# A graph layer's hot rows in three runs of matrix products, and the y products of a block's two parts in alternation

## The chip, the cores and the metric

The kernel runs on one core of a Trainium2 chip. The metric is the device time of one execution in microseconds (us). Before the change three runs took 3902.74, 3901.97 and 3891.67 us; the median is 3901.97.

The core's engines are TensorE (in the profile PE, with its weight loads PEld), VectorE (DVE), ScalarE (ACT), GpSimd (POOL) and SyncE (SP). Each takes its own instructions in order and waits on semaphores for the others. [...]

## The reference

A graph of 12,500 nodes with 128 features each and 412,500 edges, sorted by destination (every edge in both directions and one loop per node).

```python
theta = x[dst] - x[src]
w = sigmoid(relu(theta @ W1 + b1) @ W2 + b2)
agg = segment_sum(w * theta, dst)
indeg = segment_sum(ones, dst)
x = layernorm(x + agg + indeg * (x @ W4 + b4))
```

W1 and W4 are 128x128, W2 is 128x1. All is fp32.

## The kernel before, in words

**Tables.** A first stage computes `x @ W1` for all nodes into the DRAM table `z`, which holds `[x @ W1 | x]` per node, and `x @ W4 + b4` into `u_d`.

**Parts and blocks.** The edges are cut into parts of some 1,400 in the order of their destinations; the first 26 parts (`PLAIN`) have 1,024 edges and a simpler path (`early_part`, L1274). Two parts make a block (`SUB = 2`); h = 0 is its even part, h = 1 its odd one. 138 blocks come after the plain ones. The destinations of a part lie in a window of 48 nodes, those of a block in 96.

**Three kinds of work for a part.**

- *Gathered rows.* For most edges POOL gathers the source's row of `z`, 128 edges at a time: eight indirect DMAs for a part into one of seven `zbuf` buffers (`gather`, L362; DMA at L373). The destination's side `y = x[dst] @ W1 + b1` needs no gather: a one-hot matrix `oh` (48 nodes and one row for b1, in a half of 64 partitions) times the window's rows. That is `spread_y`, L845, with its matmul at L861: four products of 64 rows for a part, into one PSUM buffer `y`. There are two such buffers. VectorE then takes `y - z` (L895), the relu with W2 (L900) and the sum (L906); this is `logits`, L880.
- *Hot rows.* Edges whose source lies among the first 6,144 nodes can, up to 16 per part and table of 256 nodes, be served without a gather: the tables lie in SBUF (`tabs`), ScalarE builds a one-hot `of` from a list of their numbers (`hot_tiles`, L977; L983 and L985), and TensorE multiplies tables by one-hots (`hot_products`, L987; L997) into `pd`, which ScalarE copies to `xT_all` (`hot_out`, L1003; L1011). One such step serves four tables for eight parts; six steps fall on eight parts, so that every even part has one, and every second odd part.
- *Hot rows of a block* (`hot_rows`, L1027). From `xT_all`, where the hot edges' source rows stand transposed, TensorE makes for six tiles of 128 edges (three for each part) both `x` and the logit's operand `y - x @ W1`. `wni` is `[-W1 | identity]`, 128x256: one product with it (L1037) writes `[-x @ W1 | x]` side by side, and a second one (L1041) adds the destination's `y` from `oh`. The first part's y product uses its 64 rows; the second's uses all 128 rows, with a copy of the window's rows (`y2b`) whose first half is zero. Four of the six tiles lie in the PSUM tile `px` of two banks, two in `pz` (`hot_px`, L1021). VectorE reads the first half of each tile (`hot_logits`, L1044; L1050), ScalarE weighs the second (`hot_weights`, L1056; L1061).

**Sums.** `add_block` (L1103; matmul at L1083) adds a block's weighted rows to its 96 nodes by further one-hots, 30 instructions of TensorE, and carries what belongs to the next block. An fp32 product is two matmul instructions in the profile, each with a weight load; a transpose is one.

**The order** is written out by hand in `part(s)`, L1345, since TensorE, VectorE and ScalarE run their instructions in the order of the code there. For TensorE:

- even part of block b: y products of the first part of block b+1 (`spread_ahead`, L1336), `add_block(b - 1)`, hot products;
- odd part of block b: y products of the second part of block b+1, hot products if it has any, `hot_rows(b + 1)`.

ScalarE rebuilds `of` for the next hot products at the end of a part (`fetch_step`, L1257), after it has weighed that part's rows (L947), and only once the last hot products have read `of`.

**The gathers' pace.** `spread_ahead` also issues the gathers of part s + 3. The first of the eight waits for `newest[0]`, TensorE's latest product of a kind that records itself there when the gather is issued: `hot_rows`, `hot_products` and the sums do, `spread_y` doesn't. So in an even part the gathers wait for the block's last hot-row product, and in an odd part for the last product of the even part.

Of the kernel before, what the change touches and what calls it, by code (L numbers as in the profile page):

```python
# [9 lines left out]
F32 = mybir.dt.float32  # L10
# [69 lines left out]
def gnn_resnorm(  # L80
# [606 lines left out]
    with tc.manual_schedule(engines={SP}), tc.tile_pool(name="work", bufs=2) as wp, tc.tile_pool(  # L687
# [157 lines left out]
        def spread_y(s):  # L845

            d = parts[s]
            d["y"] = []
            for k0 in range(0, K if s < PLAIN else J, J):
                y = y_tile() if s < PLAIN - 1 else ps_y.tile([P, G, D], F32, name="y")  # L850
                d["y"].append(y)
                if s < NH:
                    px = wide().rearrange("p (k e) -> p k e", e=P)
                    for j in range(J):
                        nc.tensor.transpose(px[:, j, :], rows_of(s)[:, k0 + j, :], ident)
                    xT = next_xT()
                    nc.scalar.activation(xT, px[:, :J, :], AF.Copy)
                if NH <= s < PLAIN:
                    nc.tensor.matmul(y, away_i, rows_of(s)[:, k0:k0 + J, :D], start=True, stop=False)
                for j in range(J if s < PLAIN else pairs(s)):  # L860
                    last = nc.tensor.matmul(y[:, j, :], d["oh"][:, (k0 + j) * P:(k0 + j + 1) * P],  # L861
                                     y_of(s), start=not NH <= s < PLAIN,
                                     stop=s >= PLAIN or s >= NH and j == J - 1)
                    if s < NH:
                        last = nc.tensor.matmul(y[:, j, :], xT[:, j, :], wneg, start=False, stop=True)
            return last

# [153 lines left out]
        def hot_px(b, q):  # L1021

            n = 2 * P * G // (2 * D)
            t = (blocks[b]["px"] if q < n else pz).rearrange("p (q i d) -> p q i d", i=2, d=D)
            return t[:, q % n]

        def hot_rows(b):  # L1027

            s = b * SUB
            blocks[b]["px"] = wide()  # L1030
            j = (s - PLAIN) % HX
            xT = xT_all[:, j:j + SUB, :]
            for h in range(SUB):
                for q in range(HQ):
                    to = hot_px(b, h * HQ + q)
                    at = slice(q * P, (q + 1) * P)
                    nc.tensor.matmul(to, xT[:, h, at], wni, start=True, stop=False)  # L1037
# [3 lines left out]
                    newest[0] = nc.tensor.matmul(to[:, 0, :], oh[:, BP + q * P:BP + (q + 1) * P], y,  # L1041
                                                 start=False, stop=True)

        def hot_logits(b):  # L1044
# [3 lines left out]
            for q in range(SUB * HQ):  # L1048
                h = wp.tile([P, D], F32, name="hh", bufs=1)
                nc.vector.scalar_tensor_tensor(  # L1050
                    h, hot_px(b, q)[:, 0, :], 0.0, w2_r, op0=OP.max, op1=OP.mult,
# [4 lines left out]
        def hot_weights(b):  # L1056
# [3 lines left out]
            for q in range(SUB * HQ):  # L1060
                nc.scalar.activation(wx[:, q, :D], hot_px(b, q)[:, 1, :], AF.Copy, scale=wx[:, q, D:D + 1])  # L1061
# [212 lines left out]
        def early_part(s):  # L1274
# [24 lines left out]
            for t in range(s + 1, s + 2 if s + 1 < PLAIN else s + 3):  # L1299
                spread_y(t)  # L1300
# [35 lines left out]
        def spread_ahead(s):  # L1336

            if s + 2 < NS:
                spread_y(s + 2)
                if PLAIN + AHEAD <= s + 3 < NS:  # L1340
                    if s >= PLAIN + 4:
                        paced[s + 3] = newest[0]
                    gather(s + 3)

        def part(s):  # L1345
# [28 lines left out]
            if h == 1 and b + 1 < NK:  # L1374
                hot_rows(b + 1)
# [236 lines left out]
```

## Time and profile before

| | |
|---|---|
| median of three runs | 3901.97 us |
| profiled execution, its own time | 3876.16 us |
| its span, first to last instruction | 3874.4 us |
| mean granted TensorE clock | 0.80 |
| HBM read, written | 406.12 MB, 27.33 MB |
| DMA engines, mean over the span | 113 GB/s |

The profiled execution is one run of its own; the three timed runs stand beside it.

How to read the lines that follow. A line of a timeline has the start and the length in us, the engine, the line of the kernel, the operation with output and inputs, the shape and the count of instructions merged, and in brackets the idle time of the engine before it with what ended it. "issue" is time in which the engine waited for nothing that the profile shows, "remote" a release whose source the profile cannot name. A line of the waits has who waited for whom, and then the us in total, the number of times and the longest. Matmuls are pipelined, so the next one starts before the length of the last is over: differences of starts tell what one costs. A shape such as 64\*128 is 64 rows of weights by 128 columns, followed by the moving operand. PE is listed with its matmuls alone; weight loads run beside them.

### The profile page before, as it was taken

The page shows a single profiled execution, that of the slowest core. Times are in us where ns is not written, and L with a number is a line of the kernel's source. Part 1 is how long each engine was busy: PE and PEld are TensorE (multiplying, and loading weights), DVE is VectorE, ACT ScalarE, POOL GpSimd, SP SyncE. Part 2 cuts the span into 40 slices and gives each one's busy share as a digit, 9 for nine tenths or more (in the row PEclk, how much of TensorE's full clock was granted, in tenths as well). Part 3 has the DMA queues.
Part 4 walks back from the last instruction along what each step waited for, and adds up shares of the span by engine and source line. Part 5 has one row for each costly group of instructions (what it writes and reads, how often), then busy time and mean ns, then how long its engine had stood idle before and what let it go on. Part 6 is the DMA issues. An engine that isn't in the chain of part 4 may idle for free.

```text
span 3874.4 us, 54748 instructions
## 1 busy us (share of the span) xinstructions
PE 3062.4 (79%) x14964; PEld 2380.6 (61%) x14964; DVE 2567.2 (66%) x5694; ACT 2126.0 (55%) x5542; POOL 2322.7 (60%) x2421
## 2 busy tenths in 40 slices
PE   6786578787888878888888877788887887888887
PEld 5564466666666666666666666666666666666665
DVE  6445257776776776777657776776577777765555
ACT  5454455555555555555555554556555555565553
POOL 5444436666666666666666666666666666666663
PEclk9686778877778877878887778888888878788877
DMA  7332224443444434444444433444444444444432
GB/s 270 106 105 76 80 71 111 112 113 107 115 114 122 115 108 110 111 116 113 115 123 112 111 109 107 117 115 116 117 115 112 110 110 116 114 115 115 116 110 65
DMA packets 259984, 437.28 MB, mean 113 GB/s; under 512 B 69817, under 2 KB 177800, under 8 KB 258132
## 3 DMA queue, kind: packets, MB, share of 16 engines
q0 software_dynamic: 114752, 312.11, 29.0%
q1 hardware_dynamic: 142946, 115.19, 10.8%
q10 hardware_dynamic: 1970, 6.40, 0.5%
q8 instruction: 121, 1.98, 0.2%
q14 instruction: 195, 1.60, 0.1%
HBM read 406.12 MB, written 27.33 MB: 112 GB/s over the span
## 4 chain that ended last, share of the span: by engine, by line
PE 48%; ACT 16%; issue 14%; another core or an unknown queue 13%; DVE 7%; POOL 1%; DMA 1%; SPq 0%; DVEq 0%; POOLq 0%; ACTq 0%
PE pa L1083 10%; PE pd L997 10%; PE px L1037 9%; PE px L1041 5%; PE y L861 5%; ACT of L983 3%; PE pz L1037 3%; ACT of L985 2%; ACT wxh L1061 2%; ACT wx L947 2%; PE pz L1041 2%; ACT xT L1011 1%; DVE hh L1050 1%; DVE zbuf L895 1%
## 5 line engine op out<-in xcount | busy, mean ns | idle before, releaser
L373 POOL DMA_INDIRECT zbuf<-z,src_i x2204 | 2117.7, 961 | 1319.8 <-issue 516.8
L997 PE MATMUL pd<-of,tabs 128*128 128x128 f32 (+1 forms) x3392 | 587.0, 333 | 341.9 <-ACT xT L1011 175.9
L997 PEld LDWEIGHTS pd<-of,tabs 128*128 128x128 f32 x3392 | 534.9, 243 | 380.1 <-ACT xT L1011 194.6
L940 DVE TENSOR_TENSOR wx<-zbuf,fix 128x512 f32<-128x512 f32 x276 | 189.3, 686 | 686.8 <-ACT fix L912 665.4
L983 ACT ACTIVATE of<-hot_src,nodes 128x512 f32<-128x512 f16 (+2 forms) x424 | 281.7, 701 | 654.5 <-remote 327.4
L861 PE MATMUL y<-y,oh 64*128 64x128 f32 x2484 | 467.1, 321 | 212.3 <-issue 180.7
L1083 PE MATMUL pa<-wx,ow 128*96 128x260 f32 (+1 forms) x2620 | 597.8, 380 | 37.3 <-issue 34.8
L861 PEld LDWEIGHTS y<-y,oh 64*128 64x128 f32 x2484 | 368.9, 214 | 319.0 <-issue 252.9
L1037 PE MATMUL px<-wni,xT 128*128 128x256 f32 x1104 | 537.8, 580 | 10.0 <-issue 5.0
L1083 PEld LDWEIGHTS pa<-wx,ow 128*96 128x96 f32 x2620 | 412.9, 170 | 171.4 <-issue 42.4
L1011 ACT ACTIVATE xT<-pd 128x512 f32<-128x512 f32 (+7 forms) x347 | 131.5, 415 | 457.8 <-remote 268.5
L1041 PEld LDWEIGHTS px<-y,oh 64*128 64x128 f32 (+1 forms) x1104 | 237.4, 252 | 229.9 <-issue 213.6
L947 ACT ACTIVATE wx<-zbuf,wx 128x128 f32<-128x128 f32 x1100 | 349.5, 388 | 0.0
L895 DVE TENSOR_TENSOR zbuf<-y,zbuf 128x1024 f32<-128x1024 f32 (+1 forms) x276 | 336.4, 1219 | 13.5 <-PE y L861 7.8
L900 DVE SCALAR_TENSOR_TENSOR zbuf<-zbuf,fix 128x1024 f32<-128x1024 f32 (+1 forms) x277 | 336.5, 1215 | 10.7 <-DVE zbuf L895 0.8
L906 DVE TENSOR_REDUCE lg<-zbuf 128x8 f32<-128x1024 f32 (+1 forms) x277 | 334.6, 1208 | 4.8 <-issue 0.2
L1041 PE MATMUL px<-y,oh 64*128 64x128 f32 (+1 forms) x1104 | 335.5, 395 | 1.7 <-issue 1.1
L1037 PEld LDWEIGHTS px<-wni,xT 128*128 128x128 f32 x1104 | 231.8, 261 | 99.3 <-issue 60.2
L373 POOL DMA_INDIRECT zbuf<-z,src x144 | 137.1, 952 | 152.8 <-ACT wx L930 111.8
L1050 DVE SCALAR_TENSOR_TENSOR hh<-px,w_r 128x128 f32<-128x128 f32 x552 | 160.1, 290 | 100.7 <-PE px L1041 60.8
L985 ACT ACTIVATE of<-of 128x1024 f32<-128x1024 f32 (+2 forms) x212 | 219.7, 1036 | 6.5
L1083 PE MATMUL pa<-wxh,owh 128*96 128x130 f32 x1656 | 208.9, 274 | 17.4 <-issue 17.4
(266 smaller groups left out, 4181.0 us busy)
## 6 DMA issues: line engine op xcount, KB each, us to landing
zbuf<-z,src_i POOLq DMA_INDIRECT x2204
to_all<-off_d SPq DMA_DIRECT2D x276, 112.0 KB
hot_src<-hot_s SPq DMA_DIRECT2D x182, 128.0 KB
z<-zbuf SPq DMA_DIRECT2D x12, 1024.0 KB
xw<-in_x_dram SPq DMA_DIRECT2D x151, 48.0 KB
u<-u_d SPq DMA_DIRECT2D x151, 48.0 KB
out_dram<-o SPq DMA_DIRECT2D x151, 48.0 KB
y<-z SPq DMA_DIRECT2D x294, 24.0 KB
```

The costliest lines, as they stand in the source:

```text
L373: ins = nc.gpsimd.indirect_dma_start(out=rows_of(s)[:, k, :], out_offset=None, in_=z if s >= NH else x, in_offset=IndirectOffsetOnAxis(ap= ...
L861: last = nc.tensor.matmul(y[:, j, :], d["oh"][:, (k0 + j) * P:(k0 + j + 1) * P], y_of(s), start=not NH <= s < PLAIN, stop=s >= PLAIN or s ...
L895: nc.vector.tensor_sub(half, yy.to_broadcast([P, 2, n, D]), half)
L900: nc.vector.scalar_tensor_tensor(h[:, at, :], h[:, at, :], 0.0, w2.to_broadcast([P, n, D]), op0=OP.max, op1=OP.mult)
L906: nc.vector.tensor_reduce(lg[:, at, 0], h[:, at, :], AX.X, OP.add)
L947: nc.scalar.activation(wx[:, k, :D], rows_of(s)[:, k, D:], AF.Copy, scale=wx[:, k, D:D + 1])
L983: nc.scalar.activation(of[:, t, :], hot_src[:, i % NU, :w], AF.Abs, bias=nodes[:, t:t + 1])
L985: nc.scalar.activation(of, of, AF.Relu, scale=-1.0, bias=1.0)
L997: newest[0] = nc.tensor.matmul(to[:, q], tabs[:, g * RG + q, t, :], of[:, t, q], start=t == 0, stop=t == HT - 1)
L1037: nc.tensor.matmul(to, xT[:, h, at], wni, start=True, stop=False)
L1041: newest[0] = nc.tensor.matmul(to[:, 0, :], oh[:, BP + q * P:BP + (q + 1) * P], y, start=False, stop=True)
L1083: newest[0] = nc.tensor.matmul(to if len(w.shape) == 3 else to[:, 0, :], one, w, start=first and i == 0, stop=last and i == len(terms) - 1)
```

## The change

Two things are rearranged on TensorE; VectorE's, ScalarE's and POOL's instructions stay the same in number and size.

- `hot_rows` no longer goes tile by tile. It runs all six x tiles as transposes of `xT_all`, then the six W1 products (128x128), then the six y products. All y products use 64 rows now, and the two parts take turns, tile by tile. The PSUM layout changes with it: the first part's logit operands lie in one bank of `px`, the second's in the other; four x tiles lie in `pz`, and one in what is left of each bank of `px`.
- `spread_y` serves the plain parts alone. `spread_pair(b + 1)` makes the y products of both parts of a block, taking turns, into both `y` buffers; it stands in the odd part of block b, between the hot products and `hot_rows`. The gathers stay where they were.

```diff
@@ spread_y, now for the plain parts alone
-            for k0 in range(0, K if s < PLAIN else J, J):
+            for k0 in range(0, K, J):
...
+        def spread_pair(b):
+
+            ys = []
+            for h in range(SUB):
+                y = ps_y.tile([P, G, D], F32, name="y")
+                parts[b * SUB + h]["y"] = [y]
+                ys.append(y)
+            for j in range(J):
+                for h, y in enumerate(ys):
+                    s = b * SUB + h
+                    if j < pairs(s):
+                        nc.tensor.matmul(y[:, j, :], parts[s]["oh"][:, j * P:(j + 1) * P], y_of(s),
+                                         start=True, stop=True)
...
-        def hot_px(b, q):
-
-            n = 2 * P * G // (2 * D)
-            t = (blocks[b]["px"] if q < n else pz).rearrange("p (q i d) -> p q i d", i=2, d=D)
-            return t[:, q % n]
+        def hot_y(b, h, q):
+            return blocks[b]["px"][:, h * P * G + q * P:h * P * G + (q + 1) * P]
+
+        def hot_x(b, i):
+
+            if i < G:
+                return pz[:, i * P:(i + 1) * P]
+            return hot_y(b, i - G, HQ)
...
@@ hot_rows
-            for h in range(SUB):
-                for q in range(HQ):
-                    to = hot_px(b, h * HQ + q)
-                    at = slice(q * P, (q + 1) * P)
-                    nc.tensor.matmul(to, xT[:, h, at], wni, start=True, stop=False)
-                    oh, y = parts[s + h]["oh"], y_of(s + h)
-                    if h:
-                        oh, y = blocks[b]["oh"], blocks[b]["y2b"]
-                    newest[0] = nc.tensor.matmul(to[:, 0, :], oh[:, BP + q * P:BP + (q + 1) * P], y,
-                                                 start=False, stop=True)
+            tiles = [(h, q) for h in range(SUB) for q in range(HQ)]
+            for i, (h, q) in enumerate(tiles):
+                nc.tensor.matmul(hot_x(b, i), xT[:, h, q * P:(q + 1) * P], ident,
+                                 start=i % G == 0 or i > G, stop=False, is_transpose=True, skip_group_check=True)
+            for h, q in tiles:
+                nc.tensor.matmul(hot_y(b, h, q), xT[:, h, q * P:(q + 1) * P], wneg,
+                                 start=False, stop=False, skip_group_check=True)
+            for q in range(HQ):
+                for h in range(SUB):
+                    newest[0] = nc.tensor.matmul(
+                        hot_y(b, h, q), parts[s + h]["oh"][:, BP + q * P:BP + (q + 1) * P],
+                        y_of(s + h), start=False, stop=True, skip_group_check=True)
...
@@ hot_logits, hot_weights: read hot_y(b, *divmod(q, HQ)) and hot_x(b, q)
...
@@ early_part, at the last plain part: spread_pair(PLAIN // SUB) for two spread_y
...
         def spread_ahead(s):
 
-            if s + 2 < NS:
-                spread_y(s + 2)
-                if PLAIN + AHEAD <= s + 3 < NS:
-                    if s >= PLAIN + 4:
-                        paced[s + 3] = newest[0]
-                    gather(s + 3)
+            if PLAIN + AHEAD <= s + 3 < NS:
+                if s >= PLAIN + 4:
+                    paced[s + 3] = newest[0]
+                gather(s + 3)
...
@@ part
             if h == 1 and b + 1 < NK:
+                spread_pair(b + 1)
                 hot_rows(b + 1)
```

More of the change, by code (lines that the diff above doesn't have):

```diff
@@ L1298, in early_part @@
             logits(s)
-            for t in range(s + 1, s + 2 if s + 1 < PLAIN else s + 3):
-                spread_y(t)
+            if s + 1 < PLAIN:
+                spread_y(s + 1)
+            else:
+                spread_pair(PLAIN // SUB)
             gate_sums(s)
```

11 lines of the change are left out of this document (5 added, 6 removed).

## The prediction

> **What bounds the kernel now.** The first view is the head of the page: the span, and the busy time of the engines.
>
> ```profile
> span 3874.4 us, 54748 instructions
> PE 3062.4 (79%) x14964; PEld 2380.6 (61%) x14964; DVE 2567.2 (66%) x5694; ACT 2126.0 (55%) x5542; POOL 2322.7 (60%) x2421
> ```
>
> No engine is full, so the order of waits decides. A block past the plain ones has two parts, and each part issues eight gathers on POOL. The first gather of an even part (h = 0) waits for the last hot-row product of the block; the first gather of an odd part (h = 1) waits for the last product of the even part, in most parts a hot product (L997). The waits of POOL, and POOL's timeline over one block (start, length, count, idle time before and its releaser):
>
> ```profile
> POOL zbuf L373 <- issue: 556.5, 1802, 1.9
> POOL zbuf L373 <- PE pz L1041: 262.7, 97, 45.7
> POOL zbuf L373 <- remote: 196.1, 90, 2.7
> POOL zbuf L373 <- PE pd L997: 177.6, 43, 6.8
> ```
>
> ```profile
> 1912.09 0.94 POOL L373 DMA_INDIRECT zbuf<-z,src_i  x1 [2.04 <-PE pz L1041]
> 1913.34 0.95 POOL L373 DMA_INDIRECT zbuf<-z,src_i  x1 [0.30 <-issue]
> ...
> 1920.84 0.95 POOL L373 DMA_INDIRECT zbuf<-z,src_i  x1 [0.30 <-issue]
> 1923.88 0.94 POOL L373 DMA_INDIRECT zbuf<-z,src_i  x1 [2.10 <-remote]
> ...
> 1932.69 0.95 POOL L373 DMA_INDIRECT zbuf<-z,src_i  x1 [0.30 <-ACT oh L837]
> 1936.03 0.94 POOL L373 DMA_INDIRECT zbuf<-z,src_i  x1 [2.40 <-PE pz L1041]
> ```
>
> The gathers start 1.25 us apart (1912.09, 1913.34), eight of them end 9.7 us after the first (1920.84 + 0.95), and POOL then waits 2.0 to 2.4 us. This block takes 1936.03 - 1912.09 = 23.94 us, of which 20 are gathers. So what the change can give is bounded by those gaps, 4 us in 24, however much it takes from TensorE.
>
> TensorE's timeline over the same block, and ScalarE's:
>
> ```profile
> 1911.37 1.16 PE L861 MATMUL y<-y,oh 64*128 64x128 f32 x8
> 1912.46 3.75 PE L1083 MATMUL pa<-wx,ow 128*96 128x260 f32 x16
> ...
> 1917.60 1.95 PE L997 MATMUL pd<-of,tabs 128*128 128x128 f32 x16
> 1919.39 0.60 PE L676 MATMUL px<-wni,ew 128*128 128x128 f32 x4
> ...
> 1922.01 0.58 PE L861 MATMUL y<-y,oh 64*128 64x128 f32 x3 [0.82 <-issue]
> 1926.62 3.78 PE L997 MATMUL pd<-of,tabs 128*128 128x128 f32 x16 [4.03 <-ACT xT L1011]
> 1930.20 0.89 PE L1037 MATMUL px<-wni,xT 128*128 128x256 f32 x2
> ...
> 1931.44 0.70 PE L1037 MATMUL px<-wni,xT 128*128 128x256 f32 x2
> ...
> 1932.48 0.70 PE L1037 MATMUL px<-wni,xT 128*128 128x256 f32 x2
> ...
> 1934.28 0.60 PE L1037 MATMUL pz<-wni,xT 128*128 128x256 f32 x2
> ...
> 1934.94 0.60 PE L1037 MATMUL pz<-wni,xT 128*128 128x256 f32 x2
> ...
> 1935.68 0.49 PE L861 MATMUL y<-y,oh 64*128 64x128 f32 x2
> ```
>
> ```profile
> 1923.61 1.33 ACT L983 ACTIVATE of<-hot_src,nodes 128x512 f32<-128x512 f16 x2 [7.58 <-remote]
> ```
>
> The even part's hot products are issued by 1919.39, but ScalarE, which rebuilds `of` for the next ones, starts only at 1923.61, and POOL at 1923.88: about 1.8 us after the eighth gather ended (1921.79), whatever TensorE did. Then ScalarE, 16 hot products (to 1930.20) and the hot rows (5.48 us, to 1935.68) stand in a row, and the next gather follows at 1936.03. In this odd part the hot rows end last.
>
> **What the change removes and adds.** A tile of the first part of a block, with 64 rows, takes 1932.48 - 1931.44 = 1.04 us; one of the second, with 128 rows, 1934.94 - 1934.28 = 0.66. The products are as many, so 0.38 is what going to 64 rows and back costs. [...]
>
> At the full clock an instruction of 128 columns takes 0.112 us (16 in 1919.39 - 1917.60 = 1.79), a 64-row one no less (8 in 1912.46 - 1911.37 = 1.09, mode changes in it), and a transpose, which is one instruction where a product is two, about the same (the four of L676 fill 0.60). After the change the hot rows are 6 transposes, 12 instructions of W1 and 12 of y, with one change in and out: 30 x 0.112 + 0.38 = 3.7 us, or 3.1 if the halves overlap, against 3 x 1.04 + 3 x 0.66 = 5.1. The y products of both parts are 16 x 0.112 + 0.38 = 2.2 us, or 1.3 overlapped, against two runs of 8 x 0.112 + 0.38 = 1.28. TensorE saves 1.8 to 3.3 us a block, 240 to 455 us in 138 blocks. I take the middle of the overlap: hot rows 3.4, y pair 1.75.
>
> Where that lies on the path differs with the odd part. **With hot products in it** (half of the 138): the second part's y products used to stand where TensorE waited for ScalarE anyway (to 1922.59); they now come after the hot products, ahead of the hot rows, with the first part's beside them. The stretch from 1930.20 to the end becomes 1.75 + 3.4 = 5.15 for 5.48, with ends of 4.4 and 5.9. How much of an earlier end reaches POOL, another block shows:
>
> ```profile
> 1339.32 0.94 POOL L373 DMA_INDIRECT zbuf<-z,src_i  x1 [5.66 <-PE pd L997]
> ...
> 1348.08 0.95 POOL L373 DMA_INDIRECT zbuf<-z,src_i  x1 [0.30 <-ACT of L983]
> 1351.19 0.94 POOL L373 DMA_INDIRECT zbuf<-z,src_i  x1 [2.17 <-PE y L861]
> ```
>
> ```profile
> 1348.38 0.39 PE L1041 MATMUL pz<-y,oh 128*128 128x128 f32 x2
> ```
>
> The hot rows ended at 1348.77, before the eighth gather did, and the next gather still came at 1351.19, 11.87 us after the first; above it was 12.15. So the gain is capped at 0.28; I take 0.25: 69 x 0.25 = 17 us.
>
> **Without hot products** the odd part has TensorE at half its clock:
>
> ```profile
> 2091.29 1.22 PE L1037 MATMUL px<-wni,xT 128*128 128x256 f32 x2
> ...
> 2101.04 1.34 PE L861 MATMUL y<-y,oh 64*128 64x128 f32 x8
> ...
> 2107.71 0.27 PE L997 MATMUL pd<-of,tabs 128*128 128x128 f32 x1
> ...
> 2114.01 2.95 PE L997 MATMUL pd<-of,tabs 128*128 128x128 f32 x13 [1.73 <-issue]
> ```
>
> ```profile
> 2091.25 0.94 POOL L373 DMA_INDIRECT zbuf<-z,src_i  x1 [2.04 <-remote]
> ...
> 2101.85 0.95 POOL L373 DMA_INDIRECT zbuf<-z,src_i  x1 [0.30 <-issue]
> ...
> 2117.23 0.94 POOL L373 DMA_INDIRECT zbuf<-z,src_i  x1 [5.42 <-PE pd L997]
> ```
>
> The hot rows take 9.75 us there (2091.29 to 2101.04); at doubled prices the new ones take 6.0 to 7.3, the pair 2.4 to 4.2. They end earlier. But this very case shows the trap: they ended before the eighth gather, POOL went on without a gap, and the hot products of the next part stalled until the second eight were through; the two parts took 25.98 us instead of 23.94. POOL's waits for L997 count such cases: 43 waits at the usual 2.1 would be 90 us, there are 177.6, and the excess of 87 at 5.42 - 2.1 each makes 26 of 69. Mean now: (26 x 25.98 + 43 x 23.94) / 69 = 24.7. After the change all 69 may run so, but the eight y products ahead of the stalled hot products are gone, so eight fewer of these are left behind the stall, at 2.95 / 13 = 0.23 each: 25.98 - 1.8 = 24.2. Gain 0.5 x 69 = 35 us; the cost of that cover, if the 1.8 does not come, is the rival below.
>
> VectorE's L895 needs those y products and used to run 5 us before the hot rows were done; it now waits for the pair.
>
> ```profile
> 1930.28 1.23 DVE L895 TENSOR_TENSOR zbuf<-y,zbuf 128x1024 f32<-128x1024 f32 x1
> ...
> 1939.40 1.22 DVE L895 TENSOR_TENSOR zbuf<-y,zbuf 128x1024 f32<-128x1024 f32 x1
> ```
>
> ```profile
> DVE wx L940 <- ACT fix L912: 665.4, 138, 12.2
> ```
>
> Behind it in VectorE's queue stand the rest of the logits, the hot logits, and through them ScalarE's weights. At worst it starts at 1935.4, 5.1 us later. VectorE's later idle time for the gate is 665.4 / 138 = 4.8 us a block, so this is just covered; I cost it at nothing, and at 0.3 us a block if it is not. The pair itself waits for the odd part's L895, which frees the second y buffer: that ran at 1939.40, 3.4 us after the even part's first gather, and the hot rows began 18.1 us after it (1930.20 - 1912.09), so up to 14 us are left. Behind the pair on TensorE stand the hot rows, and for them wait the next gathers. What the DMA queues issue does not change; the gathers stay paced by the same products.
>
> **Sum.** 17 + 35 = 52 us, from the profiled 3876.2 to 3824. The median of the runs, 3902.0, is 25.8 above the profiled execution, so 3850.
>
> **The rivals.** (1) *All is hidden* behind the 11.9 us between first gathers: 3902, within 12 us of it. For it speaks the block of 1339; against it the 26 long cases. (2) *The gathers run through*, slower: the hot rows end before the eighth gather in all 69 odd parts without hot products, and the next hot products stall as at 2107.71 to 2116.96 with nothing saved. Price 69 x (25.98 - 24.7) = 88 us: 3990. It decides from hot rows that end under 9.7 us after the first gather. (3) *The halves do not overlap* and the change does not do what its second part says: 5.9 for 5.48 in the odd parts with hot products, 69 x 0.42 = 29 us later, and nothing won elsewhere: 3931. (4) *TensorE is the bound after all*, since it holds 48% of the chain on the page:
>
> ```profile
> PE 48%; ACT 16%; issue 14%; another core or an unknown queue 13%; DVE 7%; POOL 1%; DMA 1%; SPq 0%; DVEq 0%; POOLq 0%; ACTq 0%
> ```
>
> Then 240 us or more come back: 3660. Against it stand 20 us of gathers in 23.94. (5) *The clock stays at half* through a run that opens with six transposes: hot rows of at least 6.0 us for 5.48 in the odd parts with hot products, 36 us or more: 3940. Against it, 3.6 us of hot products and the pair come right before the transposes. [...]
>
> **Chances.** My forecast 0.39; (1) 0.13; (2) 0.18; (3) 0.15; (4) 0.10; (5) 0.05. A measurement of this kernel can tell about 0.3% from no change, 12 us. Faster: 0.39 + 0.10 = 0.49; same 0.13; slower 0.38. The likeliest case alone spans 3800 to 3885. The range must take in (2), (3) and (5) as well: 3780 to 3990, and leaves out (4) and the edges.
>
> **What would show it.** Hot rows of 3.1 to 3.7 us where the clock is full; a y pair under 1.9 (overlap) or of 2.2 (none); first gathers 11.9 us apart after odd parts with hot products; POOL's waits for L997 of about 3.6 us, not 5.4. The prediction is wrong if POOL's gaps grow, if VectorE's wait for the y pair reaches the gate, or if blocks come under 22 us.

## The result, and the profile after

Over 20 runs each, the kernel after the change takes 3885.8 us (3870.49 to 3893.3) and the kernel before 3903.39 us (3891.67 to 3916.84): a ratio of 0.9951, with a 95% interval of 0.994 to 0.9963. A second set of runs gave 3886.73 us against 3901.84, 0.9967 (0.9952 to 0.9983). So the change takes some 15 to 18 us away where 52 were forecast. The direction was right, and the size about a third.

The head of the page after the change, and its chain of waits by engine:

```profile
span 3875.8 us, 56094 instructions
PE 2445.5 (63%) x15792; PEld 2080.0 (54%) x15792; DVE 2570.0 (66%) x5694; ACT 2136.0 (55%) x5542; POOL 2324.0 (60%) x2421
DVE 29%; another core or an unknown queue 23%; ACT 16%; issue 15%; PE 13%; POOL 2%; DMA 2%; DVEq 0%; SPq 0%; POOLq 0%; ACTq 0%
```

TensorE's busy time fell by 3062.4 - 2445.5 = 617 us, more than any step of the prediction gave it, and its share of the chain from 48% to 13%. The span did not move: 3874.4 and 3875.8 us. The chain now names "an unknown queue" for 23%. The waits after the change:

```profile
POOL zbuf L373 <- remote: 399.5, 180, 3.2
POOL zbuf L373 <- PE px L1058: 241.1, 68, 43.5
POOL zbuf L373 <- PE pd L1010: 16.0, 4, 4.6
ACT of L996 <- remote: 407.8, 76, 8.5
DVE zbuf L908 <- remote: 275.5, 58, 6.0
DVE wx L953 <- ACT fix L925: 381.5, 128, 8.4
```

POOL still has a gap ahead of each part's first gather, and most of these gaps have lost their named releaser: 180 by "remote" for 90 before. TensorE finishes, and nobody moves.

One block shows how. It is the block of the prediction; its parts' first gathers come at 1904.68, 1916.77 and 1929.72, so 12.09 and 12.95 us apart, for 11.79 and 12.15 before. TensorE's timeline, then POOL's:

```profile
1905.76 1.95 PE L1010 MATMUL pd<-of,tabs 128*128 128x128 f32 x16
...
1919.51 3.77 PE L1010 MATMUL pd<-of,tabs 128*128 128x128 f32 x16 [10.37 <-ACT xT L1024]
1923.21 1.16 PE L878 MATMUL y<-y,oh 64*128 64x128 f32 x16
1924.31 0.66 PE L1051 MATMUL pz<-wni,xT 128*128 128x128 f32 x4
...
1925.02 1.17 PE L1054 MATMUL px<-wni,xT 128*128 128x128 f32 x9
1926.74 0.35 PE L1054 MATMUL px<-wni,xT 128*128 128x128 f32 x1 [0.56 <-issue]
1928.14 0.40 PE L1054 MATMUL px<-wni,xT 128*128 128x128 f32 x2 [1.05 <-issue]
1928.47 0.94 PE L1058 MATMUL px<-y,oh 64*128 64x128 f32 x12
```

```profile
1904.68 0.94 POOL L373 DMA_INDIRECT zbuf<-z,src_i  x1 [2.18 <-remote]
...
1913.42 0.95 POOL L373 DMA_INDIRECT zbuf<-z,src_i  x1 [0.30 <-issue]
1916.77 0.94 POOL L373 DMA_INDIRECT zbuf<-z,src_i  x1 [2.40 <-remote]
...
1925.57 0.95 POOL L373 DMA_INDIRECT zbuf<-z,src_i  x1 [0.30 <-issue]
1929.72 0.94 POOL L373 DMA_INDIRECT zbuf<-z,src_i  x1 [3.20 <-PE px L1058]
```

The even part's sixteen hot products (L1010) end by 1907.71. ScalarE waits for them to rebuild `of`, and POOL for its next gather. ScalarE's row, and the share of the DMA engines in half microseconds (the last two columns are that share and GB/s):

```profile
1916.49 1.33 ACT L996 ACTIVATE of<-hot_src,nodes 128x512 f32<-128x512 f16 x2 [6.55 <-remote]
```

```profile
1915.00:1915.50 0.50, 0.00 (x0) 0.50 0.69 164
1915.50:1916.00 0.50, 0.00 (x0) 0.50 0.26 98
1916.00:1916.50 0.50, 0.00 (x0) 0.50 0.00 0
```

They start 8.8 and 9.1 us after the products' end, just after the last transfer of the eight gathers (1916.0). By the profile the products themselves were not late: TensorE's last instruction before these rows (L676, four transposes) ends at 1909.15, none runs in them, and its granted clock, 1.00 while the products ran, is 0.50 there (the column ahead of the DMA share). What came late was the news of them. The same with the y pair: sixteen products in 1924.31 - 1923.21 = 1.10 us, and VectorE, which needs them,

```profile
1928.31 1.23 DVE L908 TENSOR_TENSOR zbuf<-y,zbuf 128x1024 f32<-128x1024 f32 x1 [5.11 <-remote]
```

starts 3.9 us after their end, when the next eight gathers are through. The trace's semaphore events let this be counted. Call a TensorE instruction on time if TensorE's semaphore rises within 0.06 us of its end in the profile. With gathers in flight, 178 of 1,092 are on time before the change and 139 of 896 after; with none in flight, 215 of 260 before. The edges of "in flight" shift such counts by some per cent, and a rise that the trace doesn't hold counts as late: the trace of before holds 1,551 rises of TensorE's semaphore for 1,815 instructions that raise it, and 2,159 of VectorE's for 4,240. So the waits must decide. After the change, 446 waits of over 0.4 us in the blocks end with a semaphore's rise whose source the profile can't name; all 446 are waits for TensorE's semaphore, alone or with others, and none is for VectorE's or ScalarE's alone. So it is TensorE's signals that come late.

The second thing to see is TensorE's "issue" gaps of 0.56 and 1.05 us within L1054, where it waits for nothing that the profile shows. They appear after 16 + 16 + 6 + 9 = 47 matmul instructions since the last landing (the last transfer of a part's eight gathers), and end at the next one. Of the 66 odd parts with hot products in this profile 61 have such a stop. It begins after 42 to 61 instructions, 47 at the median, and ends 0.15 us after the landing at the median.

**Theory A**, formed from this: while a part's gathers are in flight, most of TensorE's signals are held back, many to the landing, and TensorE itself stops some 45 to 60 matmul instructions after the last landing. So a part lasts eight gathers of 1.25 us and some 2 us of landing and signals, however short TensorE's work is; and the pair, put behind the hot products, pushes the hot rows into the stop. **Rival B**: the longer list of the new hot rows (30 instructions for 24) is what costs. **Rival C**: VectorE's late subtraction of `y` (L908) costs. **Rival D**: the chain of TensorE, ScalarE and VectorE sets the 12 us, and the gathers fit into it.

### The profile page after: what moved, and what is told of

Its sections match the earlier page's. It is cut to its first block, busy times and chain, and to the rows that moved or that the text cites. A ratio compares the mean times of both kernels' runs of the same rounds, so it can differ in the third digit from the quotient of the medians.

```text
span 3875.8 us, 56094 instructions
## 1 busy us (share of the span) xinstructions
PE 2445.5 (63%) x15792; PEld 2080.0 (54%) x15792; DVE 2570.0 (66%) x5694; ACT 2136.0 (55%) x5542; POOL 2324.0 (60%) x2421
## 4 chain that ended last, share of the span: by engine, by line
DVE 29%; another core or an unknown queue 23%; ACT 16%; issue 15%; PE 13%; POOL 2%; DMA 2%; DVEq 0%; SPq 0%; POOLq 0%; ACTq 0%
DVE zbuf L913 5%; DVE zbuf L908 5%; DVE lg L919 4%; DVE hh L1068 4%; ACT wxh L1079 3%; PE pa L1101 3%; ACT wx L960 3%; ACT of L996 2%; PE pd L1010 2%; POOL zbuf L373 2%; ACT of L998 2%; DVE ow L888 2%; ACT xT L1024 1%; DVE ew L555 1%
## 5 line engine op out<-in xcount | busy, mean ns | idle before, releaser
L1010 PE MATMUL pd<-of,tabs 128*128 128x128 f32 (+1 forms) x3392 | 557.0, 330 | 779.3 <-ACT xT L1024 681.1
L1010 PEld LDWEIGHTS pd<-of,tabs 128*128 128x128 f32 x3392 | 523.6, 242 | 799.2 <-ACT xT L1024 696.5
L1101 PE MATMUL pa<-wx,ow 128*96 128x260 f32 (+1 forms) x2620 | 610.2, 386 | 31.1 <-issue 17.9
L908 DVE TENSOR_TENSOR zbuf<-y,zbuf 128x1024 f32<-128x1024 f32 (+1 forms) x276 | 336.3, 1218 | 338.9 <-remote 275.5
L953 DVE TENSOR_TENSOR wx<-zbuf,fix 128x512 f32<-128x512 f32 x276 | 189.2, 686 | 399.7 <-ACT fix L925 381.5
L878 PE MATMUL y<-y,oh 64*128 64x128 f32 x2204 | 277.4, 362 | 264.2 <-issue 255.7
L878 PEld LDWEIGHTS y<-y,oh 64*128 64x128 f32 x2204 | 222.5, 252 | 309.0 <-issue 288.1
L1068 DVE SCALAR_TENSOR_TENSOR hh<-px,w_r 128x128 f32<-128x128 f32 x828 | 240.1, 290 | 139.9 <-remote 113.7
L1054 PE MATMUL px<-wni,xT 128*128 128x128 f32 x1656 | 280.8, 321 | 60.3 <-issue 59.9
L1054 PEld LDWEIGHTS px<-wni,xT 128*128 128x128 f32 x1656 | 260.9, 238 | 68.9 <-issue 68.5
L1101 PE MATMUL pa<-wxh,owh 128*96 128x130 f32 x1656 | 227.3, 277 | 78.5 <-issue 76.9
L1101 PEld LDWEIGHTS pa<-wxh,owh 128*96 128x96 f32 x1656 | 204.5, 164 | 108.8 <-issue 93.3
L925 ACT ACTIVATE fix<-lg,b_c 128x8 f32<-128x8 f32 (+1 forms) x276 | 74.7, 271 | 325.1 <-issue 179.6
```

Source lines behind the costliest of these rows:

```text
L878: nc.tensor.matmul(y[:, j, :], parts[s]["oh"][:, j * P:(j + 1) * P], y_of(s), start=True, stop=True)
L908: nc.vector.tensor_sub(half, yy.to_broadcast([P, 2, n, D]), half)
L1010: newest[0] = nc.tensor.matmul(to[:, q], tabs[:, g * RG + q, t, :], of[:, t, q], start=t == 0, stop=t == HT - 1)
L1054: nc.tensor.matmul(hot_y(b, h, q), xT[:, h, q * P:(q + 1) * P], wneg, start=False, stop=False, skip_group_check=True)
L1068: nc.vector.scalar_tensor_tensor(h, hot_y(b, *divmod(q, HQ)), 0.0, w2_r, op0=OP.max, op1=OP.mult, accum_out=lg[:, q, :])
L1101: newest[0] = nc.tensor.matmul(to if len(w.shape) == 3 else to[:, 0, :], one, w, start=first and i == 0, stop=last and i == len(terms) - 1)
```

## The experiments

The chips differ, and the first four experiments met one of another kind. On the chips of the first profiles and of four later sets of runs, the kernel before takes 3870 to 3917 us and leaves a gap between two parts' gathers. On two chips it takes 3160 and 3168 us with no gap. These are told apart below as chips with and without gaps; each ratio is against the kernel before on the same chip.

**Chip without gaps: hot rows alone.** `spread_pair` is taken out and the old `spread_y` put back.

```diff
-                spread_pair(b + 1)
                 hot_rows(b + 1)
@@ spread_ahead
+            if s + 2 < NS:
+                spread_y(s + 2)
```

> The new hot rows, with the y products as before the change (each part's own, two parts ahead). Theory A (the place of the y pair costs: it stands behind the hot products, where TensorE's work up to the next landing of a batch of gathers gets too long for the odd parts with hot products): the first gathers after those parts come 12.0 to 12.2 us apart again, for 12.9 in the profile after the change; the pairs of parts without hot products stay at 24.4 or go up a little, since eight y products stand ahead of the hot products again. Time 3850 to 3895 us. Rival B (the 30 instructions of the new hot rows cost, for 24 before): the odd parts with hot products stay at 12.8 to 12.9, and the time is 3900 or more.

Measured: 3156.71 us, ratio 0.9995 (0.9981 to 1.0008). **Pair alone**, with the old `hot_rows` and `hot_px`:

> The y pair, with the hot rows as before the change (tile by tile). Theory A (the place of the pair costs): odd parts with hot products go to 13.0 us or more (the pair and the slower hot rows both behind the hot products), and the time is 3895 to 3930 us. Rival B (the new hot rows cost): odd parts with hot products stay at 12.1 to 12.2 as before the change, and the time is under 3885.

Measured: 3162.6 us, 1.0007 (0.9992 to 1.0022). **Pair first:**

```diff
+            if h == 1 and b + 1 < NK:
+                spread_pair(b + 1)
             if tiled:
                 opened.append((tiled[0], hot_products(tiled.pop())))
             if h == 1 and b + 1 < NK:
-                spread_pair(b + 1)
                 hot_rows(b + 1)
```

> As after the change, with the y pair ahead of the hot products, where TensorE waits for ScalarE anyway. Theory A: the odd parts with hot products go from 12.9 to 12.0 us, the others stay at 11.8 to 12.1; 69 x 0.8 = 55 us, so about 3830 us. Rival B: the 30 instructions of the hot rows stand behind the hot products as they do now, so 12.7 to 12.9 and 3875 to 3890 us. Rival C (VectorE's late subtraction, not TensorE, is what made those parts longer): as A in time, but VectorE's wait for the pair goes and the hot rows' own gaps on TensorE stay.

Measured: 3155.83 us, 0.9983 (0.9968 to 0.9999). **Six gathers:**

```diff
-        for k in slots(s):
+        for k in slots(s)[:6 if s >= PLAIN + AHEAD else None]:
```

> As after the change, with six of the eight gathers of a part, from the 31st part on (the rows of the other two are stale, so their edges are summed wrongly; all other work is there). Theory A's ground (a part is eight gathers of 1.25 us and some 2.2 us in which the signals of TensorE's work come with the landing; TensorE's own time is hidden): a part goes from 12.2 to about 9.7 us, 272 x 2.5 = 680 us less, near 3200 us, or near 3350 if VectorE (9.3 us busy a part) binds first. Rival D (the chain of TensorE, ScalarE and VectorE sets the part, gathers fill in): the time stays over 3750 us.

Measured: 2981.3 us. None of the four expectations fits, since here the gathers run without a break. (Six gathers take 179 us off where 680 were expected, so that other work binds soon after the gathers.) POOL's timeline with the hot rows alone, over the same block:

```profile
1535.73 0.94 POOL L373 DMA_INDIRECT zbuf<-z,src_i  x1 [0.30 <-ACT a L1126]
1536.98 0.95 POOL L373 DMA_INDIRECT zbuf<-z,src_i  x1 [0.30 <-ACT fix L1143]
1538.23 0.95 POOL L373 DMA_INDIRECT zbuf<-z,src_i  x1 [0.30 <-PE px L1045]
```

The gather at 1538.23 is the first of a part, released by the last hot-row product, 1.25 us after the one before it. A part takes 10.0 us, eight times 1.25. On this chip 1,000 of 1,012 TensorE instructions signal on time with gathers in flight. So the three edits give next to nothing, because the gathers alone fill the time; and the held-back signals go with the chip that a run met, and not with the kernel. What makes one chip so and another not, no run here shows.

**The change again:**

> The change itself once more, since the first four experiments ran on a chip where the kernel before takes 3160 us and a part's eight gathers follow the last part's with no gap (10.0 us a part). If this run meets such a chip: the gathers alone set the part, so the change gives nothing (ratio 0.997 to 1.002, near 3157 us). If it meets a chip like that of the first profiles (12.0 us a part): 0.995 again, near 3886 us, with the odd parts with hot products at 12.8 to 12.9 us. A rival (the change is worth its saved TensorE time wherever TensorE's signals come in time): 1 to 2% faster on a chip with 10.0 us a part.

It met a chip with gaps: 3886.73 us, 0.9967, odd parts with hot products 13.00 us at the median, 12.94 in the first profile after the change. The change itself was not timed on a chip without gaps.

**No pace** (chip with gaps, as are the next four):

```diff
-                if s >= PLAIN + 4:
-                    paced[s + 3] = newest[0]
```

> As after the change, without the wait of a part's first gather for TensorE's latest product; the gathers still wait for a free buffer. Chip with gaps (12.0 us a part): if what withholds TensorE's signals is the gathers in flight, running them on leaves longer stretches without signals, so TensorE, ScalarE and VectorE starve and the time is 3900 us or more; if the wait for TensorE is itself the cost, the parts go to 10.0 us and the time to near 3200. Chip without gaps: the wait ends before it is due, so no change, 3140 to 3170 us.

Measured: 4450.64 us against 3901.84. The waits:

```profile
POOL zbuf L373 <- DVE wx L953: 748.7, 103, 19.2
ACT of L996 <- remote: 458.7, 67, 12.4
DVE zbuf L908 <- remote: 450.7, 42, 14.9
```

POOL now runs on until it has no free buffer, and VectorE and ScalarE wait up to 14.9 and 12.4 us for TensorE's results, for 6.0 and 8.5. More gathers in flight, later signals: this is what theory A says and rival D does not. The pace, which looks like the cost, is what keeps it small.

**Hot rows alone, pair alone, pair first, once more,** with the edits above:

> The kernel of the first experiment again, for a chip with gaps between a part's gathers and the next (12.0 us a part). There, theory A (the pair's place behind the hot products costs): odd parts with hot products 12.0 to 12.3 us, pairs of parts without them 24.0 to 24.4; 3850 to 3895 us. Rival B (the 30 instructions of the new hot rows cost): odd parts with hot products 12.7 or more, 3900 us or more. On a chip without gaps: 0.999 again.

> The kernel of the second experiment again, for a chip with gaps. Theory A: odd parts with hot products 13.0 us or more, 3895 to 3930 us. Rival B: 12.1 to 12.2 there, under 3885 us. On a chip without gaps: 1.001 again.

> The kernel of the third experiment again (the y pair ahead of the hot products), for a chip with gaps. Theory A: odd parts with hot products from 12.9 to 12.0 us, 69 x 0.8 = 55 us less than after the change, about 3830 us. Rival B: 12.7 to 12.9 there, 3875 to 3890 us. On a chip without gaps: 0.998 again.

Measured: 3863.89 us, 0.9905 (0.9882 to 0.9929); 3973.28, 1.0175 (1.0149 to 1.02); 3845.11, 0.9847 (0.9822 to 0.9873). The first lies in theory A's range; the second is 43 us over it (3895 to 3930), and the third 15 us over its 3830. All three lie on theory A's side of rival B. The same block in the three, TensorE and POOL. Hot rows alone:

```profile
1929.83 1.06 PE L1038 MATMUL pz<-wni,xT 128*128 128x128 f32 x4
...
1932.49 0.94 PE L1045 MATMUL px<-y,oh 64*128 64x128 f32 x12
1933.34 0.51 PE L861 MATMUL y<-y,oh 64*128 64x128 f32 x2
```

```profile
1923.51 0.95 POOL L373 DMA_INDIRECT zbuf<-z,src_i  x1 [2.29 <-remote]
...
1935.51 0.94 POOL L373 DMA_INDIRECT zbuf<-z,src_i  x1 [2.25 <-remote]
```

The hot rows take 3.5 us, without a stop (3 of 66 such parts have one), and end 2.2 us before POOL goes on: the part is at its floor of 12.00. Pair alone:

```profile
1981.83 2.07 PE L878 MATMUL y<-y,oh 64*128 64x128 f32 x16
...
1988.80 0.38 PE L1054 MATMUL pz<-y,oh 128*128 128x128 f32 x2
```

```profile
1989.46 0.94 POOL L373 DMA_INDIRECT zbuf<-z,src_i  x1 [4.34 <-PE pz L1054]
```

The pair stands ahead of the old hot rows and pushes them past the landing: TensorE's own work ends last. Pair first:

```profile
1911.00 0.81 PE L878 MATMUL y<-y,oh 64*128 64x128 f32 x3 [0.34 <-issue]
1914.15 3.78 PE L1010 MATMUL pd<-of,tabs 128*128 128x128 f32 x16 [2.33 <-issue]
1917.72 1.06 PE L1051 MATMUL pz<-wni,xT 128*128 128x128 f32 x4
...
1920.90 0.94 PE L1058 MATMUL px<-y,oh 64*128 64x128 f32 x12
```

```profile
1911.41 0.94 POOL L373 DMA_INDIRECT zbuf<-z,src_i  x1 [2.44 <-remote]
...
1923.53 0.94 POOL L373 DMA_INDIRECT zbuf<-z,src_i  x1 [2.38 <-PE px L1058]
```

The pair (its last products are the first line) has gone into the time in which TensorE waits for ScalarE, the hot rows have no stop, and the part takes 12.12. In this profile 22 of the 66 such parts still have a stop, but it ends well ahead of POOL's next gather, and these parts are no longer than the others (12.05 and 12.06 us at the median). Rival B falls: the same 30 instructions cost nothing where the pair isn't ahead of them. Rival C falls too: it expected the stops to stay when VectorE's wait for the pair goes (L908 has no "remote" wait left here), and they shrank with it.

**No turns:** the two loops of the y products change places, in the pair and in the hot rows.

```diff
-            for j in range(J):
-                for h, y in enumerate(ys):
+            for h, y in enumerate(ys):
+                for j in range(J):
@@ hot_rows
-            for q in range(HQ):
-                for h in range(SUB):
+            for h in range(SUB):
+                for q in range(HQ):
```

> As after the change, but the two parts' y products no longer take turns: all of the first part's, then all of the second's, in the pair and in the hot rows. If turns are what makes the products overlap, the 16 of the pair go from 1.1 us to about 1.8, the 12 of the hot rows from 0.87 to about 1.3 at the full clock, and TensorE's busy time rises by 138 x 1.1 = 150 us. The time: on a chip with gaps 0 to 40 us more than after the change, since only the odd parts with hot products have TensorE's work last; on a chip without gaps no change.

Measured: 3922.02 us, one run, beside 3902.51 for before.

```profile
PE 2603.1 (66%) x15792; PEld 2238.7 (57%) x15792; DVE 2569.4 (66%) x5694; ACT 2136.0 (54%) x5542; POOL 2326.0 (59%) x2421
```

```profile
1947.61 1.71 PE L878 MATMUL y<-y,oh 64*128 64x128 f32 x16
1949.25 0.66 PE L1051 MATMUL pz<-wni,xT 128*128 128x128 f32 x4
```

The pair's 16 products take 1949.25 - 1947.61 = 1.64 us for 1.10, and TensorE is busy 2603.1 - 2445.5 = 158 us more, with 150 expected. So the turns save what the forecast's overlap of the halves was to save: the same 16 products take 0.54 us less. Behind the hot products they are worth some 3922 - 3887 = 35 us, going by this one run.

**Idle transposes** (hot rows alone, and 16 transposes more ahead of them):

```diff
-            for i, (h, q) in enumerate(tiles):
+            for i, (h, q) in [*enumerate(tiles)] * 2 + [*enumerate(tiles)][:G] + [*enumerate(tiles)]:
                 nc.tensor.matmul(hot_x(b, i), xT[:, h, q * P:(q + 1) * P], ident,
```

> The new hot rows alone (as in the first experiment), with 16 more transposes ahead of them, whose results the real ones overwrite. Theory A (TensorE stalls once it has issued some 55 to 60 matmul instructions since the last gathers landed, until the next landing): 16 hot products, 16 transposes and 30 instructions make 62 in the odd parts with hot products, as after the change; a stall of about 1 us appears in the hot rows of those parts though no y pair stands there, and they take 12.7 to 13.0 us for 12.0. Without such a limit the transposes only take their time, 1.8 us: hot rows end at 11.5 us after the part's first gather for 9.7, with no stall, and the part stays at 12.0 to 12.2.

It met a chip without gaps: 3155.07 us, beside 3167.99 for before; nothing to see. Again:

> The last experiment's 16 more transposes again, for a chip with gaps between the parts' gathers (the last one met a chip without). Theory A: 62 instructions of TensorE since the landing, so a stall of about 1 us in the hot rows of the odd parts with hot products, which take 12.7 to 13.0 us for 12.0. Without a limit by number: hot rows end at 11.5 us with no stall, parts of 12.0 to 12.2.

Measured, with gaps: 3881.62 us, beside 3881.39 for before; so with the 16 transposes nothing is left of the 38 us that the new hot rows alone gained on another chip. The same block:

```profile
1935.61 1.28 PE L1041 MATMUL px<-wni,xT 128*128 128x128 f32 x10
1937.06 0.47 PE L1041 MATMUL px<-wni,xT 128*128 128x128 f32 x2 [0.17 <-issue]
1937.46 0.94 PE L1045 MATMUL px<-y,oh 64*128 64x128 f32 x12
```

```profile
1938.71 0.94 POOL L373 DMA_INDIRECT zbuf<-z,src_i  x1 [3.22 <-PE px L1045]
```

After 16 + 22 + 10 = 48 instructions TensorE stops, though no pair stands there. Of the 66 such parts 50 have a stop; over all of them the median is 0.76 us, for the 1 us expected, and VectorE's L895 has but one wait for the y products in this profile (18.7 us). So neither the pair nor VectorE's wait is needed for a stop. The length of the part, 1938.71 - 1925.75 = 12.96 us, is no proof of the stop: in this block the stop is 0.17 us, and most of the rest is the transposes themselves. All 22 take 1935.61 - 1932.07 = 3.54 us, at a granted clock of 0.50 for more than half of it, so the 16 more cost more than the 1.8 us that was expected.

**Six gathers again:**

> Six of the eight gathers of a part, as in the fourth experiment (the rows of the other two are stale), for a chip with gaps between the parts' gathers. Theory A (TensorE's signals come with the landing of a part's gathers, so the landing paces ScalarE, VectorE and the next part): parts shorten by up to 2.5 us, to 9.7 to 10.8 us, and the time falls to 3250 to 3500 us. Rival D (the chain of TensorE, ScalarE and VectorE needs 12 us a part, and the gathers fit into it): parts stay at 11.8 us or more, 3780 us or more. On a chip without gaps: 2980 us again.

No gaps: 2975.8 us, as expected for such a chip.

> Six of eight gathers again, for a chip with gaps. Theory A (the landing paces the part): parts of 9.7 to 10.8 us, 3250 to 3500 us. Rival D (TensorE, ScalarE and VectorE need 12 us a part): 11.8 us or more, 3780 us or more.

With gaps: 3233.14 us beside 3881.39 for before, a little under the range of theory A (its parts are shorter too, 8.9 to 9.1 us for 9.7 at the least) and far from rival D.

```profile
1619.90 0.95 POOL L373 DMA_INDIRECT zbuf<-z,src_i  x1 [6.75 <-PE px L1058]
...
1626.17 0.95 POOL L373 DMA_INDIRECT zbuf<-z,src_i  x1 [0.30 <-issue]
1628.85 0.94 POOL L373 DMA_INDIRECT zbuf<-z,src_i  x1 [1.73 <-remote]
```

The last part shown takes 1628.85 - 1619.90 = 8.95 us, and the median is 8.9 to 9.1 in all but the odd parts with hot products, which take 11.0 to 11.2 (there TensorE's work ends last: a gap of 6.75 ahead of 1619.90). TensorE, ScalarE and VectorE do all their work in 9 us a part where they took 12, once fewer gathers are in flight.

**Before again,** the kernel unchanged:

> The kernel before, profiled once more: the profiled execution lay 25 us under the median of its runs. If executions differ by how many odd parts without hot products have their gathers run straight on into the next part's (two parts 26 us instead of 24), one near 3900 us shows more of them, about 12 pairs of 2 us more; if not, the odd parts with hot products or something outside the parts differ. Odd parts with hot products 12.1 to 12.2 us either way.

> The kernel before, profiled once more, for a chip with gaps (the last one met a chip without). If executions differ by how many pairs of parts without hot products take 26 us for 24, one near 3900 us shows about 12 more of them than the first profile. If not, those pairs are as many, and the difference lies in the odd parts with hot products or outside the parts.

The first met a chip without gaps (3168.77 us, 10.0 us a part at the median). The second met one with gaps, but at 3872.47 us, like the first profile, so the question stays open. The timed run beside it took 3869.91 us, so it isn't the profiling that makes an execution of before this short.

## Why the prediction was right or wrong

The starts and ends of POOL's and TensorE's rows give, for 58 of the odd parts with hot products in each profile, these medians in us after the part's first gather (pair: start to end; stop: "issue" gaps before and within the hot rows):

| kernel | pair | hot rows | their length | stop | next first gather |
|---|---|---|---|---|---|
| before | | 6.25 to 11.87 | 5.60 | 0 | 12.15 |
| after | 6.39 to 7.90 | 7.83 to 12.63 | 4.67 | 1.07 | 12.94 |
| hot rows alone | | 6.25 to 9.69 | 3.60 | 0 | 12.00 |
| pair alone | 6.39 to 7.93 | 7.87 to 13.27 | 5.36 | 0 | 13.54 |
| pair first | before them | 6.26 to 10.26 | 4.00 | 0 | 12.06 |
| no turns | 6.39 to 8.36 | 8.29 to 13.03 | 4.67 | 0.90 | 13.30 |
| idle transposes | | 6.26 to 12.58 | 6.32 | 0.76 | 12.89 |

And by two parts, odd and even, from first gather to first gather (67 pairs with hot products, 66 without):

| kernel | with hot products, mean | without, mean | without: over 25 us |
|---|---|---|---|
| before | 24.82 | 24.51 | 20 |
| after | 25.49 | 23.96 | 1 |
| hot rows alone | 24.75 | 24.37 | 14 |
| pair alone | 26.50 | 24.37 | 18 |
| pair first | 24.73 | 23.99 | 1 |

Each mean with hot products holds one pair of 64 to 74 us, at the start of the stage. Without it the means are 24.18, 24.89, 24.12, 25.78 and 24.14.

- **The bound: right.** Only POOL's gaps can be won, about 4 us in 24, and TensorE's 617 us were hidden. The prediction saw that the even part's gathers went on "whatever TensorE did" and that a part whose hot rows end early still takes 11.87 us. It used this as a cap on one term, and did not ask what else waits for the landing. In the block above, on a chip with gaps, the hot products' end in the profile and the start of ScalarE, which waits for them, lie 8.8 us apart; why gathers in flight should hold TensorE's signals back, no run here shows.
- **TensorE's prices: right, or too high.** The pair takes 1.10 us in the block above, at a granted clock of 1.00 (1.3 overlapped was forecast, 1.75 taken). The hot rows take 3.60, with 3.1 to 3.7 forecast and 3.4 taken, but in the block shown of the hot rows alone the first 1.23 us of them run at a granted clock of 0.52, with 0.85 us for the first four transposes; in a block of the hot rows alone on the chip without gaps these four take 0.44 and the hot rows 3.03 (1515.89 to 1518.92). No row of before shows the two halves at work side by side, so the overlap in the prices of 3.1 and 1.3, and with it in the 3.4 and 1.75 of the sum, was the author's estimate; the runs showed 1.10 us for the pair with turns and 1.64 without. TensorE saves 617 us, with 455 as the upper end. The hot rows alone save 3062.4 - 2712.1 = 350 us of its busy time and the pair alone 3062.4 - 2890.4 = 172.
- **The odd parts with hot products: wrong, and this step failed.** Forecast was a stretch of 1.75 + 3.4 = 5.15 us for 5.48 and a gain of 0.25 us, 17 us in all. Measured are some 1.45 for the pair and 4.67 for the hot rows, 6.1 us for 5.60; the next gather comes 0.79 later, and the pairs of parts are 25.49 - 24.82 = 0.67 us longer, 46 us in 69. Without the stop the stretch would be 1.45 + 3.60 = 5.05, as forecast. So the two prices together were right, and what the sum lacked is the stop of 1.07 us, which the profile before doesn't show in these parts at the median (16 + 24 instructions). It shows it elsewhere, partly in rows that the prediction shows: from 2107.71 to 2114.01 TensorE issues three hot products, with "issue" gaps of 2.52, 1.15 and 1.73 us. The prediction called this a stall until the gathers were through, and priced it in the parts without hot products alone. It did not ask whether a longer list behind the hot products would meet it too. The second part of the mistake is the place. Before the change the second part's y products cost nothing where TensorE waited for ScalarE; the prediction says so, and let them go behind the hot products at their full price. "Pair first" undoes this alone and takes 3886.73 - 3845.11 = 42 us off; 69 x 0.8 = 55 was expected.
- **The odd parts without: the size right, the mechanism wrong, so the size is luck.** Forecast 24.7 to 24.2 and 35 us; measured 24.51 to 23.96, 0.55 x 69 = 38 us. The 26 long pairs out of 69 were 20 out of 66, at 26.4 us. The forecast let all 69 run so, each 1.8 us shorter than such a pair was. Measured, they are gone: one is left. What breaks them up goes with the pair's place right ahead of these hot rows, since "hot rows alone" keeps 14 and "pair first" 1; but "pair alone" keeps 18, so it takes the short hot rows too. The mechanism was not isolated.
- **VectorE's wait: right in size.** It comes (L908, 275.5 us in 58 waits, 4.75 each, with "5.1 us later" as the worst forecast), though in the block above 3.9 us of it lie behind the pair's end, up to the landing, and its wait for the gate, 665.4 before, fell to 381.5. Both together are 657 us, so the cover held.
- **The signs named ahead.** The pair came under 1.9 us; the hot rows come in 3.1 to 3.7 us only without the pair ahead of them; the first gathers after odd parts with hot products are 12.94 us apart, not 11.9; and POOL's waits for the hot products (L997, now L1010) didn't shrink to 3.6 us each but nearly ceased, 4 for 43.
- **The rivals.** (1) Hidden: true of nearly all the saving, and the measured change of 15 to 18 us lies just outside its 12. (2) The gathers run through: one pair of 66. (3) No overlap: the turns do save time (1.10 us for 1.64), but a loss in the odd parts with hot products came by another way. (4) TensorE is the bound: 617 us saved there and the span unchanged. (5) The clock: the hot rows after the change run at a granted clock of 1.00, with the pair and the hot products ahead of them, in the block above. That transposes could keep the clock at half was the author's supposition; a run of 22 of them, in the idle transposes, did not. Three stretches of TensorE there, where the number before the last two is the granted clock:

```profile
1900.27:1903.68 3.41, 2.55 (x13) 2.38 (x12) 0.66 (x2) 2.03 (x9) 1.52 (x2) 0.50 0.21 52
1903.68:1907.09 3.41, 3.41 (x18) 3.41 (x17) 2.64 (x8) 3.35 (x11) 2.50 (x4) 0.50 0.39 118
1907.09:1910.00 2.91, 2.91 (x32) 2.79 (x31) 2.88 (x4) 2.88 (x4) 2.30 (x3) 1.00 0.44 114
```

  TensorE ran nothing but transposes from 1903.14 to 1907.50 (L1038), and the full clock came at 1907.09. In this profile the full clock begins 28 times after 3.41 us in which TensorE had nothing but transposes.
- **What stays open.** The two terms measured make 46 - 38 = 8 us slower, and the two profiled spans differ by 1.4, while the runs differ by 15 to 18 the other way. Both profiled executions of before (3876.16 and 3872.47 us) lie under the 3902 of most of its runs; where those spend the 25 us more, no profile shows. The second table does account for the runs of the other kernels: from after the change its means give some 23 us less for the hot rows alone, 95 more for the pair alone and 49 less for pair first, and the medians of the runs say 23, 87 and 42. Only before doesn't fit: the means put it 9 us under after the change, the runs 15 to 18 over it. So what the change costs in the odd parts with hot products is shown by the experiments, and what its whole gain of 15 to 18 us is made of is not. That the stop is set by the number of instructions is borne out by one experiment and by the counts at which stops begin (42 to 61 after the change); since pair first has stops in a third of its parts and not in the rest, the number alone doesn't settle it. What stops TensorE there was not shown.

## What to carry to other kernels

Before a shorter engine is credited, look who is released by it, and when: if the waiting engines start at the same moment whatever the producer did (here just after the last transfer of a batch), its time is not on the path. A list of instructions that costs nothing in an idle gap can cost its full time, and here more, when it is moved behind the work that ends the gap; so the better version is the one that fills the gap (pair first, 3845.11 us). And run the kernel on more than one chip before a wait is blamed on the code.

## What the runs showed of the hardware that was not expected

- The kernel before takes some 19% less on two chips (3160 and 3168 us) than on the others (3870 to 3917). In the profiles the difference is whether TensorE's signals come while gathers by POOL's indirect DMAs are in flight: 1,000 of 1,012 on time, against 178 of 1,092, and 446 waits on TensorE that end with an unnamed rise after the change, against none with the hot rows alone on the chip without gaps.
- In the profile after the change, on a chip where they don't, TensorE also stops after 42 to 61 matmul instructions since the last landing (47 at the median), until the next one, in 61 of 66 odd parts with hot products.
- Sixteen 64-row products that take turns between the two halves of the array cost 1.10 us at a granted clock of 1.00, 0.069 each; in two runs of eight, 1.64 us, 0.103 each (the four transposes behind them start over 0.49 us in the one run and 0.50 in the other).
- A stretch of 3.41 us that held nothing but fp32 transposes was followed by the full clock, 28 times in one profile (idle transposes).
